# Mixture-of-experts steps of a decoder layer: two half blocks side by side on TensorE, results in rows of their own, the down bias inside the step

## The chip, the cores and the metric

The kernel runs on one core of a Trainium2 chip. The metric is the device time of one execution in microseconds; the timed runs are given by their median. The profile is of one execution that the hardware profiler recorded. Its span runs from the first to the last instruction, and the execution's own time is a little longer than the span.

## The reference

One decoder layer on 8 sequences of 112 tokens (896 tokens, width 512), all in fp32: causal self-attention with 16 heads of 128, a linear cross-attention over 375 context rows, and a mixture of 8 experts with the 2 best taken for each token. Each part is followed by a layer norm over the sum with its input. What the change touches is the last part:

```python
logits = h @ router_weight.T + router_bias
top_vals, top_idx = jax.lax.top_k(logits, TOP_K)          # TOP_K = 2, E = 8
top_w = jax.nn.softmax(top_vals, axis=-1)
scores = jnp.zeros_like(logits).at[jnp.arange(T)[:, None], top_idx].set(top_w)
gate_up = jnp.einsum('th,ehj->etj', h, gate_up_proj) + gate_up_proj_bias[:, None, :]
gate = jnp.minimum(gate_up[..., ::2], LIMIT)
up = jnp.clip(gate_up[..., 1::2], -LIMIT, LIMIT)
act = (up + 1.0) * gate * jax.nn.sigmoid(gate * ALPHA)
expert_out = jnp.einsum('eti,eih->eth', act, down_proj) + down_proj_bias[:, None, :]
out = jnp.einsum('te,eth->th', scores, expert_out)
...
x = _layernorm(x + out, axis=-1)
```

The inputs are drawn from a fixed seed, so the number of tokens that each expert gets is fixed as well.

## The kernel before

The 896 tokens are 7 tiles of 128 rows. Attention runs first (to about 530 us of the span). Then cross-attention is woven together with routing: for a batch b the cross-attention is finished, and `close(t)` (L956) projects a tile of tokens (xops), normalizes it (LN, with a square root on ACT) and routes it. `route` (L503) transposes the tile (x2T), forms the logits (lps), takes the best two on DVE, counts with a triangular matrix (cps) at which row of the expert's region each token goes, and scatters the token twice into `store`, a DRAM array with 896 rows for each expert. A row of `store` (516 words) holds the 512 values, the first expert's number (XF), the score difference (XD), the second score (XS) and the token's number (XK).

`keep_scores` (L576) builds for each tile the sum of the token and the score-weighted down bias: a transpose by matmul (sTps), a matmul with the biases (dbps), a DVE add (sum), and a store into the DRAM array `total`.

`list_blocks` (L610) works out on DVE, with some 18 to 22 small operations, which blocks of 128 rows of `store` the next steps take, and from which expert. It runs three times: after 5 tiles for 3 steps, after 6 tiles for 2 steps, and after all for 16 steps (`LISTS`, 21 steps in all). `es` is the expert, `eb` the same in integers with the block's number and, for late steps, whether the expert differs from the step four before.

An expert step s takes one block of 128 rows. Its parts, in the order of the final loop (L1209):
- `project(s, 0)`: 4 matmuls of 128x512 with the gate weights, called gups(s,0) below; DVE adds the bias (gu), takes the minimum, ACT does the sigmoid (sg).
- the transposes of step s-1's activation (aT, copied out by ACT) and of step s+1's block (bT, copied by ACT), with `start(s+1)`, a few small DVE operations.
- `project(s, 1)`: the same with the up weights, gups(s,1); three more DVE operations finish the activation g(s).
- `down(s-1)`: 4 matmuls with the down weights (yps), ACT copies the result to y, and POOL scatters y into `total` with an accumulating DMA.

There are four weight sets ("lanes", `NQ`) of three slabs of 1 MB (gate, up, down). Step s uses lane s % 4; `fetch_weights(s+3)` on SP's queue follows `down(s-1)` and is skipped where the expert hasn't changed (from step 9 on). `fetch_tokens(s+3)` on POOL's queue loads the block xblk, right after `start(s+1)`.

The order on PE, DVE, ACT and SP is the one in which the program is written (`manual_schedule`); each engine takes its instructions in that order. `tick()` advances the generators `close` and `keep_scores` by one piece, which weaves their pieces between the steps.

The tail: after step 15's result is scattered, SP loads `total` back in 7 tiles (xn), `close_tiles` normalizes them on DVE and ACT and writes them out. Tokens of the last five steps (`LATE`) are gathered from `total`, completed with y (`close_steps`), normalized and scattered into the output; `find_again` (L1180) finds on PE and DVE which tokens appear in two late steps, so that only the last one is written. The last step's result is completed in PSUM with a matmul over step 19's y (`finish`).

Of the kernel before, what the change touches and what calls it, by code (L numbers as in the profile page):

```python
# [19 lines left out]
P = 128  # L20
# [13 lines left out]
NQ = 4  # L34


LISTS = ((5, 3), (6, 2), (NT, 16))
STEPS = 21
LATE = 5
LN_EPS = 1e-5  # L40
# [5 lines left out]
def decoder_layer(ctx: ExitStack, tc: tile.TileContext, t_in: dict, out: bass.AP):  # L46
# [41 lines left out]
    def counting(name: str, shape, pattern):  # L88
# [27 lines left out]
    place = [  # L116
        counting(f"place{n}", [P, n, E], [[1, n], [0, E]]) for _, n in LISTS[:-1]
    ]
    late = LISTS[-1][1]
    place.append(  # L120
        counting(
            "place_late",
            [P, late // NQ, NQ, E],
            [[1, late // NQ], [late // NQ, NQ], [0, E]],
        ).rearrange("p i q e -> p (i q) e")
    )
# [12 lines left out]
    total = dram.tile([T + P, D], F32, name="total")  # L139
# [5 lines left out]
        base=T,  # L145
        channel_multiplier=1,
        allow_small_or_imprecise_dtypes=True,
    )

# [14 lines left out]
    def clear(n: int):  # L164
# [6 lines left out]
        else:  # L171
            nc.sync.dma_start(out=store[E * T :, :], in_=blank)
            nc.sync.dma_start(out=total[T:, :], in_=blank[:, :D])
# [325 lines left out]
    db = const.tile([E, D], F32, name="db")  # L499
    nc.scalar.dma_start(out=db, in_=t_in["db"])  # L500
    rows = const.tile([P, NT, 2], I32, name="rows")

    def route(t: int):  # L503
# [70 lines left out]
        return first, both  # L574

    def keep_scores(t: int, first, both):  # L576

        sco = small.tile([P, E], F32, tag="sco", name=f"sco_{t}")
        yield
        nc.vector.tensor_scalar_mul(sco, both, xe[:, t, XS : XS + 1])  # L580
        nc.vector.scalar_tensor_tensor(
            sco, first, xe[:, t, XD : XD + 1], sco, ALU.mult, ALU.add
        )
        yield
        yield
        yield
        sps = bank(f"sTps_{t}", "aux")
        nc.tensor.matmul(sps[:E, :P], sco, ident, start=True, stop=True)
        sT = small.tile([E, P], F32, tag="sT", name=f"sT_{t}", bufs=2)
        nc.scalar.copy(sT, sps[:E, :P])  # L590
        yield
        yield
        dps = bank(f"dbps_{t}", "aux")
        nc.tensor.matmul(dps, sT, db, start=True, stop=True)
        first_sum = side.tile([P, D], F32, tag="sum", name=f"sum_{t}")
        nc.vector.tensor_add(first_sum, xn[:, t, :], dps)
        yield
        yield
        put = nc.sync.dma_start(out=total[t * P : (t + 1) * P, :], in_=first_sum)
        if t == NT - 1:  # L600
            tc.declare_no_dep(put.ins, group="early", reason="tokens of other tiles")
# [83 lines left out]
    with tc.tile_pool(name="cross", bufs=2) as cr:  # L685
# [211 lines left out]
        def fetch_weights(s: int):  # L897
            for fetched in fetch_in_parts(s):
                pass
# [416 lines left out]
```

## Time and profile before

| what | us |
|---|---|
| median of 3 runs (988.66 to 990.53) | 990.17 |
| the profiled execution's own time | 985.63 |
| its span | 984.0 |
| first expert matmul starts | 721.59 |
| step 18 of 21 starts (third from the end) | 932.6 |
| last matmul of step 20's up projection ends | 962.9 |
| last normalized rows ready on DVE | 976.7 |

How to read it: the profile's parts are counted from the span's start. "Busy" of PE counts overlapping matmuls once. A group line gives engine, operation, output and inputs by the program's names, then the count, the busy time and the mean duration. A matmul in fp32 appears as two records. A line of the timeline gives start, length, engine, line, operation and how many records were merged into it.

The DMA queues in brief: q1 is SP's (98.28 MB), q0 is POOL's (15.75 MB). In the 40 slices of the page the DMA engines are near full from about 713 to 812 us.

### The profile page before, as it was taken

The page shows a single profiled execution, that of the slowest core. Times are in us where ns is not written, and L with a number is a line of the kernel's source. Part 1 is how long each engine was busy: PE and PEld are TensorE (multiplying, and loading weights), DVE is VectorE, ACT ScalarE, POOL GpSimd, SP SyncE. Part 2 cuts the span into 40 slices and gives each one's busy share as a digit, 9 for nine tenths or more (in the row PEclk, how much of TensorE's full clock was granted, in tenths as well). Part 3 has the DMA queues.
Part 4 walks back from the last instruction along what each step waited for, and adds up shares of the span by engine and source line. Part 5 has one row for each costly group of instructions (what it writes and reads, how often), then busy time and mean ns, then how long its engine had stood idle before and what let it go on. Part 6 is the DMA issues. An engine that isn't in the chain of part 4 may idle for free.

```text
span 984.0 us, 10556 instructions
## 1 busy us (share of the span) xinstructions
PE 949.3 (96%) x3847; PEld 490.5 (50%) x3847; DVE 461.0 (47%) x1020; ACT 244.7 (25%) x430; POOL 185.2 (19%) x235
## 2 busy tenths in 40 slices
PE   7998999999999999999999999999889999999994
PEld 3455644466445654654555454445444444444442
DVE  1356511145213551556421757667785433333484
ACT  1132311033102321332222233333223211211132
POOL 3133300031101322211002212221111212111132
PEclk9999999999999999999999999999999999999998
DMA  8991004102011001030100111120599997692432
GB/s 337 363 343 44 1 1 171 43 5 82 0 43 43 1 1 43 30 119 0 32 1 1 32 54 43 53 65 33 193 376 335 340 393 200 218 330 43 97 88 81
DMA packets 33845, 115.08 MB, mean 117 GB/s; under 512 B 3846, under 2 KB 8006, under 8 KB 26241
## 3 DMA queue, kind: packets, MB, share of 16 engines
q1 hardware_dynamic: 26784, 98.28, 27.2%
q0 software_dynamic: 6336, 15.75, 6.5%
q8 instruction: 31, 0.51, 0.2%
q10 hardware_dynamic: 672, 0.36, 0.1%
q14 instruction: 22, 0.17, 0.1%
HBM read 115.83 MB, written 29.01 MB: 147 GB/s over the span
## 4 chain that ended last, share of the span: by engine, by line
PE 84%; DVE 9%; issue 3%; ACT 2%; POOL 1%; DMA 1%; POOLq 0%; DVEq 0%; SPq 0%; ACTq 0%
PE gups L1061 14%; PE ops L237 10%; PE yps L1087 7%; PE vps L327 6%; PE zps L435 3%; PE xqps L877 2%; PE xgps L877 2%; PE sps L387 2%; DVE z L850 2%; PE xops L237 1%; PE pps L427 1%; PE aT_ps L982 1%; PE bT_ps L982 1%; DVE p L412 1%; PE sumps L812 1%
## 5 line engine op out<-in xcount | busy, mean ns | idle before, releaser
L1061 PE MATMUL gups<-slab,bT 128*128 128x512 f32 x336 | 153.2, 599 | 2.5 <-ACT bT L986 2.5
L1061 PEld LDWEIGHTS gups<-slab,bT 128*128 128x128 f32 x336 | 62.6, 192 | 73.0 <-issue 69.4
L237 PE MATMUL ops<-slab,zT 128*128 128x512 f32 x224 | 97.9, 593 | 0.0
L1069 DVE TENSOR_TENSOR gu<-gups,biases 128x512 f32<-128x512 f32 x42 | 29.0, 691 | 116.6 <-PE gups L1061 116.4
L1087 PE MATMUL yps<-slab,aT 128*128 128x512 f32 x168 | 76.0, 595 | 2.3 <-ACT aT L986 2.3
L237 PEld LDWEIGHTS ops<-slab,zT 128*128 128x128 f32 x224 | 42.1, 190 | 50.2 <-issue 49.5
L275 POOL TENSOR_TENSOR ws<-slab 128x256 f32<-128x256 f32 x16 | 11.8, 738 | 281.7 <-PE qk_5c L291 83.0
L327 PE MATMUL vps<-slab,x0T 128*112 128x512 f32 x128 | 58.7, 613 | 1.0 <-DVE x0T L187 0.8
L1101 POOL DMA_INDIRECT total<-y,nums x19 | 30.7, 1618 | 135.0 <-ACT y L1098 61.1
L1087 PEld LDWEIGHTS yps<-slab,aT 128*128 128x128 f32 x168 | 31.3, 190 | 40.5 <-issue 37.1
L244 DVE TENSOR_TENSOR xn<-xn,ops 128x512 f32<-128x512 f32 x28 | 19.2, 685 | 55.4 <-PE ops L237 55.4
L435 PEld LDWEIGHTS zps<-pT,v 112*128 112x128 f32 x256 | 33.5, 192 | 12.3 <-issue 11.1
L442 DVE COPY zT<-zps 128x448 f32<-128x448 f32 x32 | 20.0, 624 | 39.8 <-PE zps L435 39.8
L327 PEld LDWEIGHTS vps<-slab,x0T 128*112 128x112 f32 x128 | 22.9, 184 | 31.4 <-issue 29.7
L411 DVE TENSOR_REDUCE nm<-p 112x4 f32<-112x448 f32 x32 | 19.7, 616 | 30.8 <-POOL p L401 30.8
L1098 ACT COPY y<-yps 128x512 f32<-128x512 f32 x20 | 11.7, 584 | 87.8 <-issue 79.8
L435 PE MATMUL zps<-pT,v 112*128 112x112 f32 x256 | 33.4, 273 | 0.0
L1073 ACT ACTIVATE sg<-gu 128x512 f32<-128x512 f32 x21 | 13.2, 630 | 70.6 <-DVE gu L1071 53.0
L237 PE MATMUL xops<-slab,gate 128*128 128x512 f32 x56 | 25.8, 603 | 4.1 <-DVE gate L852 3.4
L395 ACT ACTIVATE p<-sps 112x448 f32<-112x448 f32 x32 | 17.4, 544 | 45.6 <-PE sps L387 45.6
L565 POOL DMA_INDIRECT store<-xn,rows x14 | 14.0, 1000 | 75.7 <-DVE count L627 48.2
L387 PE MATMUL sps<-k,q 128*112 128x112 f32 x256 | 28.0, 262 | 0.0
(799 smaller groups left out, 1616.5 us busy)
## 6 DMA issues: line engine op xcount, KB each, us to landing
slab<-in_wg_dram SPq DMA_DIRECT2D x21, 1024.0 KB
slab<-in_wu_dram SPq DMA_DIRECT2D x21, 1024.0 KB
slab<-in_wd_dram SPq DMA_DIRECT2D x21, 1024.0 KB
store<-slab SPq DMA_DIRECT2D x8, 1806.0 KB
biases<-gubs SPq DMA_DIRECT2D x21, 512.0 KB
cT<-in_ctxT_dram SPq DMA_DIRECT2D x8, 750.0 KB
xblk<-store POOLq DMA_DIRECT2D x21, 258.0 KB, 7.7
slab<-in_wq_dram SPq DMA_DIRECT2D x4, 1024.0 KB
```

The source lines that it names most:

```text
L237: nc.tensor.matmul(ps, aT[:, c, t * P : (t + 1) * P], w[:, c, :], start=(c == 0), stop=(c == C - 1),)
L327: nc.tensor.matmul(ps[:S, :], xT[:, c, b * S : (b + 1) * S], w[:, c, :], start=(c == 0), stop=(c == C - 1),)
L387: nc.tensor.matmul(ps[:S, i * S : (i + 1) * S], qk["q"][:, rows], qk["k"][:, rows], start=True, stop=True,)
L411: nc.vector.tensor_reduce(nm, p, AX.X, ALU.max, negate=True)
L435: nc.tensor.matmul(zps[:, i * S : (i + 1) * S], v[:, half * 4 + i, hl * DH : (hl + 1) * DH], pT[:, i * S : (i + 1) * S], start=True, stop= ...
L442: nc.vector.tensor_copy(zT[:, hl, half * HALF : (half + 1) * HALF], zps[:, :HALF])
L850: nc.vector.reciprocal(zf, zf)
L877: nc.tensor.matmul(ps[:, :HALF], w[:, c, g * P : (g + 1) * P], xT[:, c, cols], start=(c == 0), stop=(c == C - 1),)
L1061: nc.tensor.matmul(ps, st["bT"][:, c, :], st["w"][k][:, c, :], start=(c == 0), stop=(c == C - 1),)
L1069: nc.vector.tensor_add(a, ps, st["bias"][:, k * I : (k + 1) * I])
L1087: nc.tensor.matmul(ps, st["aT"][:, c, :], st["wd"][:, c, :], start=(c == 0), stop=(c == C - 1 and s < STEPS - 1),)
L1101: put = nc.gpsimd.indirect_dma_start(out=total, out_offset=bass.IndirectOffsetOnAxis(ap=st["num"], axis=0), in_=y, in_offset=None, compute ...
```

## The change

The steps become 18: 5 early ones with whole blocks (as before), 8 paired steps, and 5 late ones with whole blocks. A paired step takes two half blocks of 64 rows, possibly of two experts: half 0 in rows 0 to 63, half 1 in rows 64 to 127, with two lanes of weights, (1,2) or (3,0) in turn. Each matmul of 128 stationary columns becomes two of 64, one for each half, that write the lower and the upper half of the PSUM bank's rows. `list_blocks` now runs four times: the first two as before, then twice in a row after the last tile, for the five late whole blocks and for the paired halves (whole blocks are those that are more than half full; the rest are counted in halves).

`keep_scores` and `total` go. In their place the DRAM array `parts` has two rows for each token, one for each of its experts, plus 128 for padding; each step writes its result by a plain scatter into a row of its own (num = token + 896 x "is first expert"), and the token itself is added where it is the first expert. The down bias of the step's experts is loaded (`fetch_down_bias`) and enters y on DVE: y = bias x score + PSUM, then y = token x first + y (`add_token`); the copy on ACT goes. All of `parts` is cleared in attention (15 blocks of 256 KB instead of one). At the end SP loads 14 tiles (xn and `seconds`) after step 12, and `close_tiles` adds the two. Late steps gather the other expert's row.

Loads follow lanes: `fetch_inner(s)` loads gate and up weights and the biases for step s, `fetch_down(s)` the down weights; below inner(s) and down(s). `fetch_next(s, ...)` loads what the lanes of step s need next. `fetch_tokens(s+3)` moves behind `down(s-1)`, with two loads of 64 rows in a paired step. In step 0, `close` of the last tile moves from behind the second projection to behind the first.

The diff, cut to its core:

```diff
-LISTS = ((5, 3), (6, 2), (NT, 16))
-STEPS = 21
+LISTS = ((5, slice(0, 3)), (6, slice(3, 5)), (NT, slice(13, 18)), (NT, slice(5, 13)))
+EARLY, PAIRED, STEPS = 5, 13, 18
 LATE = 5
+LANES = [(s % NQ,) for s in range(EARLY)]
+LANES += [((1, 2), (3, 0))[s % 2] for s in range(PAIRED - EARLY)]
+LANES += [(1,), (2,), (3,), (0,), (1,)]
...
-    total = dram.tile([T + P, D], F32, name="total")
+    parts = dram.tile([2 * T + P, D], F32, name="parts")
...
-            nc.sync.dma_start(out=total[T:, :], in_=blank[:, :D])
+            nc.sync.dma_start(
+                out=parts.rearrange("(n p) d -> p n d", p=P),
+                in_=blank[:, :D].unsqueeze(1).broadcast_to([P, 2 * NT + 1, D]),
+            )
...
-    def keep_scores(t: int, first, both):
...
+        def fetch_down_bias(s: int):
+            downs[s] = side.tile([P, D], F32, tag="down_bias", name=f"down_bias_{s}", bufs=2)
+            for i, (e, _) in experts_of.pop(s).items():
+                on, _ = part_of(s, i)
+                nc.sync.dma_start(
+                    out=downs[s][on],
+                    in_=t_in["db"][bass.ds(e, 1), :].broadcast_to([on.stop - on.start, D]),
+                )
...
             elif t == NT - 1:
                 list_blocks(2)
-            later.append(keep_scores(t, *first_both))
+                list_blocks(3)
...
             for c in range(C):
-                nc.tensor.matmul(
-                    ps,
-                    st["bT"][:, c, :],
-                    st["w"][k][:, c, :],
-                    start=(c == 0),
-                    stop=(c == C - 1),
-                )
+                for rows_, q in parts_of(s):
+                    nc.tensor.matmul(
+                        ps[rows_],
+                        st["bT"][:, c, rows_],
+                        slab[3 * q + k][:, c, :],
+                        start=(c == 0),
+                        stop=(c == C - 1),
+                    )
...
-            nc.scalar.copy(y, ps)
+            nc.vector.scalar_tensor_tensor(
+                y, downs.pop(s), st["score"], ps, ALU.mult, ALU.add
+            )
+            add_token(y, st)
             st["y"] = y
             if s < STEPS - 2:
-                put = nc.gpsimd.indirect_dma_start(
-                    out=total,
+                nc.gpsimd.indirect_dma_start(
+                    out=parts,
                     out_offset=bass.IndirectOffsetOnAxis(ap=st["num"], axis=0),
                     in_=y,
                     in_offset=None,
-                    compute_op=ALU.add,
-                )
+                )
             if s == STEPS - LATE - 1:
                 for t in range(NT):
-                    nc.sync.dma_start(
-                        out=xn[:, t, :], in_=total[t * P : (t + 1) * P, :]
-                    )
+                    for k, to in ((1, xn), (0, seconds)):
+                        nc.sync.dma_start(
+                            out=to[:, t, :],
+                            in_=parts[k * T + t * P : k * T + (t + 1) * P, :],
+                        )
...
             for t in range(NT):
+                nc.vector.tensor_add(xn[:, t, :], xn[:, t, :], seconds[:, t, :])
                 closing_stats(t, xn[:, t, :])
...
             if st:
                 project(s, st, 0)
+                if s == 0:
+                    settle(0)
+                    chains.append(close(NT - 1))
                 tick()
+            if s - 2 >= STEPS - LATE:
+                before_last = steps[s - 2]
+                nc.vector.tensor_add(before_last["sum"], before_last["sum"], before_last["y"])
...
-                if s >= 1 and s + 3 < STEPS:
-                    ahead_x.append(fetch_tokens(s + 3))
             if st:
                 project(s, st, 1)
-                if s == 0:
-                    settle(0)
-                    chains.append(close(NT - 1))
                 tick()
                 if s == 0:
-                    next(third)
-                    ahead_w.append(fetch_weights(3))
+                    fetch_down(2)
+                    fetch_inner(3)
+                    fetch_down(3)
+
+                if s not in (1, PAIRED):
+                    fetch_next(s, fetch_inner)
+                if s == 2:
+                    fetch_next(1, fetch_inner)
...
             if before_:
                 down(s - 1, before_)
                 tick()
-                if s - 1 + NQ < STEPS:
-                    ahead_w.append(fetch_weights(s - 1 + NQ))
+                if s == PAIRED:
+                    fetch_next(s, fetch_inner)
+                fetch_next(s - 1, fetch_down)
+                if s + 1 < STEPS:
+                    fetch_down_bias(s + 1)
+                if s + 3 < STEPS:
+                    ahead_x.append(fetch_tokens(s + 3))
```

## The prediction

> **What bounds the kernel now.** I read the page's totals first, then TensorE's order of time (the timeline of PE) around the expert steps, then the busy time by stretch, then the orders of ACT and DVE where a wait shows.
>
> ```profile
> span 984.0 us, 10556 instructions
> PE 949.3 (96%) x3847; PEld 490.5 (50%) x3847; DVE 461.0 (47%) x1020; ACT 244.7 (25%) x430; POOL 185.2 (19%) x235
> ...
> DMA packets 33845, 115.08 MB, mean 117 GB/s; under 512 B 3846, under 2 KB 8006, under 8 KB 26241
> ...
> PE 84%; DVE 9%; issue 3%; ACT 2%; POOL 1%; DMA 1%; POOLq 0%; DVEq 0%; SPq 0%; ACTq 0%
> ```
>
> TensorE is busy 96% of the span and carries 84% of the chain that ended last. So PE work that goes is time that goes, unless another engine is late in its place. One expert step, and the one place where column strips are used already:
>
> ```profile
> 716.25 1.03 PE L812 MATMUL sumps<-values,kf 125*32 125x33 f32 x96
> ...
> 758.18 1.12 PE L594 MATMUL dbps<-db,sT 8*128 8x512 f32 x2
> 759.23 3.70 PE L1087 MATMUL yps<-slab,aT 128*128 128x512 f32 x8
> 762.77 3.60 PE L1061 MATMUL gups<-slab,bT 128*128 128x512 f32 x8
> 766.20 0.60 PE L982 MATMUL aT_ps<-ident,gu 128*128 128x128 f32 x4
> 766.64 0.60 PE L982 MATMUL bT_ps<-ident,xblk 128*128 128x128 f32 x4
> 767.08 3.60 PE L1061 MATMUL gups<-slab,bT 128*128 128x512 f32 x8
> 770.51 3.60 PE L1087 MATMUL yps<-slab,aT 128*128 128x512 f32 x8
> ```
>
> By the starts a step is 3.43 + 0.44 + 0.44 + 3.43 + 3.43 = 11.18 us with no gap. A matmul is two records; 512 columns are (3.60 - 0.59) / 7 = 430 ns each. The sumps matmuls write four 32-row strips with 33 columns each: in a row these would be 430 x 33 / 512 = 27.7 ns apart, but they start (1.03 - 0.20) / 95 = 8.7 ns apart. Four strips thus ran 3.2 at a time, in fp32, each with its own moving data.
>
> ```profile
> 745.00:757.00 12.00, 12.00 (x47) 6.48 (x46) 5.55 (x21) 3.46 (x7) 1.66 (x1) 1.00 1.02 402
> 876.00:921.00 45.00, 45.00 (x132) 21.85 (x131) 16.83 (x44) 8.70 (x16) 8.07 (x7) 1.00 0.36 88
> 944.00:956.00 12.00, 12.00 (x37) 5.97 (x36) 10.55 (x28) 7.03 (x11) 3.56 (x3) 1.00 0.37 88
> 956.00:984.00 28.00, 15.43 (x42) 6.66 (x40) 14.64 (x34) 5.75 (x10) 8.77 (x8) 0.89 0.31 93
> ```
>
> The columns are PE, PEld, DVE, ACT, POOL busy, clock, DMA share, GB/s. The steps are PE-bound throughout; DMA is saturated at 402 GB/s early and idle late; DVE is nearly full (10.55 of 12) just before the end.
>
> **What the skill says.** TensorEngine Tiling (Key Properties): tiles work in parallel, and a change of tiling mode drains TensorE. The sumps line agrees on the first; its neighbours start without a visible gap, so the drain is under 0.1 us here. TensorE: Matmul & The Clock Gate (Part 3): three column tiles at N=512 gave 2.38x, matmuls are strict FIFO. If FIFO holds, a pair's low record waits for its own half and one slot of 0.43 us is lost per run. DMA: Bandwidth & Descriptors (Rules for kernel authors): two transfers to partition halves serialize, so halving xblk and the biases saves nothing; no run here shows it.
>
> **The change, part by part.** All in the profiled execution's time (span 984.0, run 985.63); the runs' median 990.17 is 4.5 us above it, and I carry the difference over.
>
> (a) Before the first expert matmul (721.6). keep_scores goes: per tile one sTps (0.31 us on PE) and one dbps (1.05), and a DVE sum (0.68). Up to 691 PE is full (157.5 of 161 us) and three tiles' worth goes: 3 x 1.36 = 4.1. Between 691 and 721.6 the chain runs through DVE as well: one sum 0.7, one dbps 1.05, one sTps partly 0.2. First gups at 715.6: -6.0. The larger clear of parts (15 blocks of 256 KB, in attention) lies under a DMA share near 0.1: nothing; if a weight load waited, some 10 us of queue, with two heads (16 heads take 530 us) before the next load.
>
> (b) Steps 0 and 1. Here the last tile's close moves ahead of the second gups, and list_blocks runs twice in a row.
>
> ```profile
> 755.48 1.28 ACT L558 ACT_TABLE_LOAD   x1
> 756.77 0.20 ACT L558 ACTIVATE ex<-d 128x1 f32<-128x1 f32 x1
> 756.88 0.57 ACT L986 COPY aT<-aT_ps 128x512 f32<-128x512 f32 x1
> ...
> 754.65 0.16 DVE L543 TENSOR_TENSOR at<-cps,upto 128x8 f32<-128x8 f32 x1
> ...
> 757.66 0.16 DVE L627 TENSOR_TENSOR count<-upto 128x8 f32<-128x8 f32 x1
> ...
> 761.15 0.15 DVE L995 CAST nums<-xblk 128x1 int32<-128x1 f32 x1
> ```
>
> Routing takes 757.66 - 754.65 = 3.0 us of DVE; the list 3.5 us for 18 operations, 0.194 each. Walk of the new order: gups(0,0) 715.6; xops waits for gate (724.2 - 5.0 = 719.2), then bT(1) and gups(0,1) end at 726.6. DVE finishes list_blocks(1) at 724.9, then gu(0), adds xops and normalizes: with two ACT table loads of 1.28 in between, xn is ready at 730.4. PE waits 3.8 (before: 2.55 at this place). x2T, gups(1,0), lps, aT, bT, gups(1,1) end at 739.5 = c. Now in DVE's queue stand gu(1) 2.8, routing 3.0, 45 list operations 8.7, y(0) 1.45, and only then gu(2,0) 1.1: c + 17.0. ACT's sg(2) (table 1.28 + 0.63) waits for that, and aT(1) (0.57) stands behind sg(2): c + 19.5. PE's own work (cps, yps(0), gups(2,0), aT, bT, gups(2,1)) lasts until c + 11.4. So yps(1) waits 8.1 us and starts at 759.0, against 759.23 before. The 6 us of (a) are given back. Bounds on this wait: 5 to 10.
>
> (c) From yps(1) to the third step from the end. Before: 759.2 to 932.6. After: yps(1) 3.43, then 12 steps x 11.18 = 134.2, keys 0.2. The three steps less are 33.5 us. Terms not in the trace:
> - Column halves: 8 paired steps with 12 pairs each. From below: fully side by side, 0. From above: one after the other, 8 x 12 x 0.86 = 82. By the sumps line each strip's matmul cost about 5.5 ns over its stream, 1% at 512 columns. I take one lost FIFO slot a step: 8 x 0.43 = 3.4.
> - Tokens: fetch_tokens(s+3) now stands behind y(s-1) and its scatter on POOL, 11 us later than before. y +1.7, scatter issue +1.2, first half's fetch +1.2, second +1: issued by +5. The view of the tile xblk, from issue to landing:
>
> ```profile
> DMA to landing us min/median/max: 2.9/7.7/12.1
> ```
>
> bT(s+3) is due at 11.18 + 3.9 = +15.1, so the median has 2 us to spare and the worst is 2 us late. Between 0 and 10 us in all; I take 1.5 us.
> - Weights: the seeded inputs route 260, 280, 188, 216, 264, 172, 200, 212 rows to the experts. Before: 13 experts are loaded (9 unconditional, 4 on change; the page's 7,604 packets of 8 KB and over agree, 384 an expert plus 20 earlier slabs). After, by the lists: 5 + 9 + 5 = 19, of 3.15 MB. Seven come within steps 5 to 8, whose slabs come free one step ahead. At 345 GB/s left for this queue, wu and wd of steps 7 and 8 land about when they are due: 0 to 7 us, I take 2.
> - Two new DVE operations a step (bias and token into y, 0.73 each) replace ACT's copy (0.58): DVE goes to some 6.3 of 11.2 us, hidden. The plain scatter instead of an accumulating one costs POOL no more than its 1.6 us.
> Third step from the end: 759.0 + 3.4 + 134.2 + 0.2 + 3.4 + 1.5 + 2 = 903.7.
>
> (d) The tail. Before: 932.6 to 984.0 = 51.4. After, DVE gets seven xn + seconds adds (0.69 each), two operations for each y and sum + y at once. In steps 15 and 16 its queue sums to 17.5 and 13.8 us against 22.4 of PE. Further, SP's 14 xn and seconds loads wait for step 12's scatter, take 3.67 MB / 300 GB/s = 12 us (290 GB/s in the stretch 929 to 935, where seven such loads run before), and behind them stand inner(17), down(15), down(16) and then the down bias of step 14: it lands 22 us into step 15, where y(14) wants it at 16.5. DVE stands 5.6 us, and behind it gu(16,0), sg, aT(15). Adding DVE's queue from there: g(16) at 35, sg(17) at 43.7, yps(16) 44.3 to 47.7, last scale at 57.3, against 44.1 before: 64.6 to the end. Bounds: 56 (bias in time, DVE covered) to 70.
>
> **Sum.** 903.7 + 64.6 = 968.3, 15.7 less than 984.0. On the median: 990.17 - 15.7 = 974.5 us.
>
> **Rivals.**
> 1. As summed: 974.5, own range 964 to 986. Chance 0.69.
> 2. Slower: the halves do not overlap for 512 columns. Place: gups and yps of the eight paired steps. Price: up to 82 - 3.4 = 79 us, 1053; decided once a pair costs over (15.7 + 3.4) / 82 = 23% more than one full matmul. For: no 64-column half is in the trace, and 33-column strips are short. Against: 3.2 streams at once were sustained there. Chance 0.12, spread between 990 and 1053.
> 3. Transfers bind in the paired steps: tokens 1 us late in each (8) and weights 4 more: 986. For: DMA share 1.02 at 402 GB/s early, 6 experts more. Against: the load is light in steps 9 to 12. Chance 0.11.
> 4. The tail's queue is absorbed (14 loads early, bias in time): 8 to 11 us better, 964. Against: DVE's sum alone fills two steps. Chance 0.08.
>
> **Numbers.** What can be told from no change is 0.2%, 2 us. Faster: 0.69 x 0.98 + 0.11 x 0.6 + 0.08 = 0.82, taken at 0.80; same 0.04; slower 0.16 (rival 2 and the end of 3). The range 961 to 997 leaves out most of rival 2 and a little below.
>
> **What would show it.** Right: gups of a paired step with 16 records in about 3.5 to 3.9 us; 18 steps; no dbps; a PE wait of some 8 us for ACT aT L1022 before the second yps; DVE over 0.9 busy in the last 45 us and PE waiting there on aT. Wrong: 16 records in 6.9 us; PE waits on xblk or slab in steps 5 to 9 above 10 us together; or a tail no longer than before.

## The result, and the profile after

The changed kernel is slower: 995.71 us median against 989.06 for the kernel before, ratio 1.0072 with a 95% interval of 1.0054 to 1.009. Forecast were 974.5 us and "faster". The profiled execution (993.77 us) has a span of 992.2 us (before 984.0, summed in the prediction 968.3). Cut into four stretches, the span shows where the forecast and the chip part. Steps begin with their first gups; step 3 is the fourth of the 18.

| stretch (us) | before | predicted | after | after less predicted |
|---|---|---|---|---|
| start to first gups | 721.6 | 715.6 | 720.9 | +5.3 |
| first gups to start of step 3 | 41.2 | 46.8 | 47.1 | +0.3 |
| step 3 to third step from the end | 169.8 (15 steps) | 141.3 (12 steps) | 155.1 | +13.8 |
| from there to the end | 51.4 | 64.6 | 69.2 | +4.6 |

The page after, in the same lines as were read before:

```profile
span 992.2 us, 10895 instructions
PE 925.1 (93%) x3915; PEld 468.3 (47%) x3915; DVE 481.1 (48%) x1053; ACT 226.9 (23%) x394; POOL 173.8 (18%) x239
...
DMA packets 39653, 142.35 MB, mean 143 GB/s; under 512 B 4438, under 2 KB 8598, under 8 KB 29744
...
PE 61%; DVE 13%; issue 12%; DMA 9%; ACT 2%; POOL 1%; POOLq 0%; SPq 0%; DVEq 0%; ACTq 0%
```

TensorE lost 24.2 us of work (949.3 to 925.1), but the span grew by 8.2: TensorE's share of the chain that ended last fell from 84% to 61%, and DMA's rose from 1% to 9%. The bytes grew by 27.3 MB. Packets of 8 KB and over are 39,653 - 29,744 = 9,909, which is 2,305 more than before: six experts at 384 packets each are 2,304, as the lists said (19 loads against 13).

TensorE's order of time after (start, length, group, and in brackets the idle time before it with what ended it):

```profile
720.85 6.17 PE L1120 MATMUL gups<-slab,bT 128*128 128x512 f32 x8
...
761.99 6.09 PE L1147 MATMUL yps<-slab,aT 128*128 128x512 f32 x8 [5.95 <-ACT aT L1022]
...
815.77 3.65 PE L1120 MATMUL gups<-slab,bT 128*64 128x512 f32 x14 [1.04 <-DMA slab<-in_wg_dram]
...
822.85 3.65 PE L1120 MATMUL gups<-slab,bT 128*64 128x512 f32 x14 [1.41 <-DMA slab<-in_wu_dram]
829.40 3.97 PE L1147 MATMUL yps<-slab,aT 128*64 128x512 f32 x16 [2.90 <-ACT aT L1022]
...
846.37 6.08 PE L1147 MATMUL yps<-slab,aT 128*64 128x512 f32 x13 [3.75 <-DMA slab<-in_wd_dram]
...
864.19 3.60 PE L1120 MATMUL gups<-slab,bT 128*64 128x512 f32 x16
867.72 0.65 PE L1018 MATMUL aT_ps<-ident,gu 128*128 128x128 f32 x4
868.21 0.60 PE L1018 MATMUL bT_ps<-ident,xblk 128*128 128x128 f32 x4
868.74 3.65 PE L1120 MATMUL gups<-slab,bT 128*64 128x512 f32 x16
872.23 3.60 PE L1147 MATMUL yps<-slab,aT 128*64 128x512 f32 x16
875.66 3.60 PE L1120 MATMUL gups<-slab,bT 128*64 128x512 f32 x16
...
956.21 0.77 PE L1249 MATMUL keys<-sums,allones 128*128 128x128 f32 x2 [13.89 <-DVE closing L217]
956.77 5.90 PE L1147 MATMUL yps<-slab,aT 128*128 128x512 f32 x8
```

Three things are to be seen. First, the lines from 864.19 to 875.66 are one undisturbed paired step: 11.47 us, and 16 records of 64 columns take 3.60 to 3.65 us, what 8 records of 128 took before. The halves run side by side; a paired step costs 0.29 us more than a whole one (11.18). Second, the waits: 5.95 us before the second yps (forecast 8.1), then steps 7 and 8, from 813.71 to 851.55, which take 19.8 and 18.1 us, since TensorE waits there for gate, up and down weights and for aT, and 13.9 us in step 16. Third, groups of eight matmuls that take 6.1 instead of 3.6 us: TensorE at about half its clock, mostly after such a wait. The mean clock granted is 0.58 while gups(0,0) runs (from 720.85), 0.59 for yps(1), 0.50 for the thirteen records from 846.37 and 0.60 for the yps from 956.77.

The stretches (PE, PEld, DVE, ACT, POOL busy, clock, DMA share, GB/s), first after, where 820 to 880 stands once whole and once in its two halves, then before:

```profile
760.00:820.00 60.00, 56.97 (x198) 23.65 (x199) 25.97 (x54) 8.78 (x16) 10.66 (x16) 0.94 1.02 346
820.00:880.00 60.00, 51.81 (x228) 18.79 (x226) 22.71 (x49) 6.37 (x12) 7.85 (x11) 0.94 0.90 280
820.00:850.00 30.00, 21.81 (x89) 7.89 (x88) 9.43 (x22) 3.18 (x6) 2.10 (x3) 0.92 1.02 312
850.00:880.00 30.00, 30.00 (x143) 10.90 (x140) 13.28 (x27) 3.18 (x6) 5.75 (x8) 0.96 0.79 247
880.00:935.00 55.00, 54.17 (x203) 23.44 (x202) 32.01 (x83) 7.96 (x15) 7.05 (x9) 1.00 1.00 385
```

```profile
820.00:880.00 60.00, 60.00 (x173) 28.92 (x172) 20.07 (x51) 11.46 (x21) 12.43 (x11) 1.00 0.75 245
880.00:935.00 55.00, 55.00 (x161) 26.81 (x160) 21.88 (x58) 10.87 (x20) 8.06 (x7) 1.00 0.36 80
```

The DMA engines, slack from 880 on before, are full after (share 0.99 to 1.03) from 760 to 850, in which steps 7 and 8 wait, and again from 880 to 940; from 850 to 880 the share is 0.79. In the tail DVE's own order shows the late bias:

```profile
939.33 0.16 DVE L1259 TENSOR_TENSOR again<-again,twice 128x3 f32<-128x3 f32 x1
946.60 0.75 DVE L1158 SCALAR_TENSOR_TENSOR y<-down_bias,score,yps 128x512 f32<-128x512 f32 x1 [7.11 <-DMA down_bias<-in_db_dram]
```

### The profile page after: what moved, and what is told of

Its sections match the earlier page's. It is cut to its first block, busy times and chain, and to the rows that moved or that the text cites. A ratio compares the mean times of both kernels' runs of the same rounds, so it can differ in the third digit from the quotient of the medians.

```text
span 992.2 us, 10895 instructions
## 1 busy us (share of the span) xinstructions
PE 925.1 (93%) x3915; PEld 468.3 (47%) x3915; DVE 481.1 (48%) x1053; ACT 226.9 (23%) x394; POOL 173.8 (18%) x239
## 2 busy tenths in 40 slices
DMA packets 39653, 142.35 MB, mean 143 GB/s; under 512 B 4438, under 2 KB 8598, under 8 KB 29744
## 4 chain that ended last, share of the span: by engine, by line
PE 61%; DVE 13%; issue 12%; DMA 9%; ACT 2%; POOL 1%; POOLq 0%; SPq 0%; DVEq 0%; ACTq 0%
PE ops L254 10%; PE vps L344 6%; DMA parts<-y,nums 5%; PE zps L452 3%; PE xqps L888 2%; PE xgps L888 2%; DVE z L861 2%; PE sps L404 2%; PE xops L254 1%; DMA down_bias<-in_db_dram 1%; PE pps L444 1%; DVE p L429 1%; PE sumps L823 1%; DVE kf L783 1%; PE kvps_0a L769 1%
## 5 line engine op out<-in xcount | busy, mean ns | idle before, releaser
L1120 PE MATMUL gups<-slab,bT 128*64 128x512 f32 (+1 forms) x416 | 136.2, 603 | 2.6 <-DMA slab<-in_wu_dram 1.4
L1147 PE MATMUL yps<-slab,aT 128*64 128x512 f32 (+1 forms) x208 | 74.4, 650 | 14.5 <-ACT aT L1022 9.9
L1120 PEld LDWEIGHTS gups<-slab,bT 128*64 128x64 f32 (+1 forms) x416 | 48.7, 160 | 73.2 <-issue 68.8
L1128 DVE TENSOR_TENSOR gu<-gups,biases 128x512 f32<-128x512 f32 x36 | 24.8, 689 | 73.6 <-PE gups L1120 56.6
L1147 PEld LDWEIGHTS yps<-slab,aT 128*64 128x64 f32 (+1 forms) x208 | 27.1, 173 | 55.9 <-issue 38.5
L1164 POOL DMA_INDIRECT parts<-y,nums x16 | 16.5, 1033 | 158.8 <-DVE y L1185 144.2
L1158 DVE SCALAR_TENSOR_TENSOR y<-down_bias,score,yps 128x512 f32<-128x512 f32 x17 | 12.7, 747 | 32.6 <-PE yps L1147 24.6
L412 ACT ACTIVATE p<-sps 112x448 f32<-112x448 f32 x32 | 17.4, 544 | 45.6 <-PE sps L404 45.6
```

The costliest lines, as they stand in the source:

```text
L1120: nc.tensor.matmul(ps[rows_], st["bT"][:, c, rows_], slab[3 * q + k][:, c, :], start=(c == 0), stop=(c == C - 1),)
L1128: nc.vector.tensor_add(a, ps, st["bias"][:, k * I : (k + 1) * I])
L1147: nc.tensor.matmul(ps[rows_], st["aT"][:, c, rows_], slab[3 * q + 2][:, c, :], start=(c == 0), stop=(c == C - 1 and s < STEPS - 1),)
```

## The experiments

All medians, with the ratio to the kernel before run on the same chip. m1, m2, a1 and t3 leave out work that the result needs; they only price it.

| run | us | ratio, 95% interval |
|---|---|---|
| m1_no_weights_7_8 | 979.26 | 0.9916, 0.9884 to 0.9947 |
| m2_no_biases_7_8 | 988.33 | 0.9995, 0.9976 to 1.0015 |
| b1_bias_before_up | 999.48 | 1.0112, 1.0076 to 1.0148 |
| m3_reversed | 980.92 | 0.9898, 0.9859 to 0.9937 |
| t1_bias_before_sums | 995.26 | 1.0071, 1.0046 to 1.0096 |
| t2_bias_sums_weights | 992.15 | 1.0011, 0.9987 to 1.0035 |
| s1_lists_apart | 994.16 | 1.0057, 1.0034 to 1.008 |
| a1_no_keep_scores | 980.91 | 0.9921, 0.9892 to 0.995 |
| c1_three_orders | 978.91 | 0.9894, 0.9851 to 0.9937 |
| c2_adds_on_pool | 977.0 | 0.9875, 0.9835 to 0.9915 |
| d1_filled_waits | 981.17 | 0.9908, 0.9871 to 0.9944 |
| e1_orders_pool_filled | 987.27 | 0.9998, 0.9978 to 1.0019 |
| f1_sums_later | 977.92 | 0.9879, 0.9857 to 0.9902 |
| t3_no_second_adds | 978.46 | 0.9889, 0.9868 to 0.9911 |
| g1_short_fillers | 972.62 | 0.9837, 0.9816 to 0.9859 |

### The loads of steps 7 and 8

Weights left out (m1, in `fetch_inner` and in `fetch_down`):

```diff
                     e, cond = chosen[i]
+                    if s in (7, 8):
+                        continue
```

> The changed kernel without the loads of gate, up and down weights for steps 7 and 8 (three experts by the lists, 9.4 MB); the biases are still loaded, and steps 7 and 8 compute with the weights left in their slabs. Theory A (the bytes of the weights bind the first paired steps): steps 7 and 8 fall from 19.8 and 18.1 to 11.5 to 12.5 us each, DVE's waits on the biases go as well, and the time falls by 13 to 16 us to about 981. Rival E (the paired steps wait for something else, the biases or the tokens): steps 7 and 8 stay above 15 us. The gap between step 16 and 17 stays at 28 us in any case.

Measured: 11.47 and 11.48 us for the two steps, together 14.9 less; the time is 16.5 below the changed kernel's. In the stretch view of this run:

```profile
760.00:820.00 60.00, 57.55 (x206) 24.17 (x208) 27.98 (x63) 10.16 (x18) 11.12 (x17) 0.94 0.95 317
820.00:880.00 60.00, 60.00 (x296) 21.96 (x294) 28.14 (x63) 8.62 (x17) 9.43 (x13) 1.00 0.70 246
```

From 820 to 880 TensorE is busy throughout, the DMA share 0.70 instead of 0.90. Without these 9.4 MB nothing stops steps 7 and 8. The waits for the biases went with them, so m1 alone does not divide the 14.9 us between weights and biases.

Biases left out (m2, the same two lines in the loop over the biases), and biases issued earlier (b1):

```diff
+            load(0, "wg")
+            if not EARLY <= s < PAIRED:
+                load(1, "wu")
             for i in parts_:
...
+            if EARLY <= s < PAIRED:
+                load(1, "wu")
```

> The changed kernel without the loads of the gate and up biases for steps 7 and 8 (at most four times 256 KB); the weights are loaded as before, and the two steps add the biases left in their rows. Theory A (the weights' bytes bind; the biases are late because they stand behind them): the waits of 2.9 and 3.75 us for ACT's aT go, but TensorE then waits on the slabs instead; steps 7 and 8 together fall from 37.9 us by 0 to 4 us. Rival E (the place of the biases behind the weights is what costs): steps 7 and 8 fall by 7 to 10 us together, since the two aT waits and one yps at half clock go.

> The changed kernel (lanes in their first order) with the gate and up biases of the paired steps issued between the gate and the up weights instead of behind both; nothing is left out. Theory E (the place of the biases behind the weights costs: without them steps 7 and 8 fell by 8.4 us): the two aT waits (2.9 and 3.75 us) and the yps at half clock go, steps 7 and 8 together fall from 37.8 to 30 to 33 us, the time by 4 to 8 us. Theory A alone (only bytes count, and what goes at the biases comes back at the up weights): 36 us or more, and the time stays within 2 us of the changed kernel's.

Without the biases the two steps fell by 8.4 us to 29.4, as theory E had it; with the biases ahead of the up weights they still took 36.3. The wait of 2.9 us for aT was gone, but TensorE now waited 2.9 us for gate, 1.5 for up and 2.5 for down weights (1.0, 1.4 and 3.8 in the changed kernel: the 3.75 us that both expectations give to aT were a wait for down weights, by the line at 846.37). The time did not fall (999.48; its interval overlaps with the changed kernel's). So giving the biases this earlier place gains nothing: what goes at the biases comes back at the weights. Left out in m2 were 142.35 - 141.56 = 0.79 MB, 2 to 3 us at the 280 to 346 GB/s of that stretch; the rest of the 8.4 would be the steps behind a late bias (DVE, ACT, aT) and one yps at half clock, which is argued and not shown. Whether loads into 64 of the 128 rows are slower for their size was not measured.

The lanes' halves in reverse order (m3), which changes no result, only when which expert is due:

```diff
-            pattern=[[1, (PAIRED - EARLY) // 2], [PAIRED - EARLY, 2], [0, E]],
-            base=half * (PAIRED - EARLY) // 2,
+            pattern=[[-1, (PAIRED - EARLY) // 2], [PAIRED - EARLY, 2], [0, E]],
+            base=(half + 1) * (PAIRED - EARLY) // 2 - 1,
```

> The changed kernel with each lane's four half blocks taken in the reverse order. The halves and the results are the same; by the lists three experts fewer are loaded for steps 7 and 8 (one instead of three for step 7 and none, since a lane now starts with the expert it has most halves of), three instead of one for steps 11 and 12, and none for step 13: 18 experts instead of 19. Theory A (bytes due in steps 7 and 8 bind): these two steps fall from 37.8 us to 23 to 25, and what was gained is kept, since the loads of steps 11 and 12 come when the queue is light: 980 us (977 to 984). Rival F (the queue is short of bytes over the whole stretch from step 5 to step 16, so that a wait only moves): steps 7 and 8 fall as much, but waits on slabs of 8 us or more appear in steps 11 to 16 and the time stays at 988 or more.

Measured: steps 7 and 8 take 11.47 us each, no step from 7 to 15 takes more than 11.74, and the stretch from step 3 to step 15 is 138.0 us (155.1 in the changed kernel, 141.3 forecast). The time falls by 14.8 us. Two things changed at once, the spread of the loads (three experts were due in two steps) and their number (one less, 139.20 MB); no run parts them.

This profile had luck as well. Its first gups came only at 728.6, behind groups at half clock (below), and step 3 at 775.6, 7.7 us later than in the changed kernel, so that the loads had more time. In the seven other runs with the reversed halves (all of which change other orders too) step 3 starts between 761.0 and 768.8, waits for weights stand again, above all at the end of step 6 (2.2 us or more) and in steps 11 to 13, and the stretch to step 15 lasts 144.4 to 150.6 us. That is still less than the 153.6 to 157.1 us of the five programs with all loads and the first order. So theory A holds for steps 7 and 8; F as it was put falls (no such waits in m3, and 981 instead of 988 us), but transfers still hold these steps once they come earlier.

### The tail

The 14 sums' loads behind bias and weights (t1), or the bias first, then sums, then weights (t2):

```diff
                 if s == STEPS - LATE:
+                    fetch_down_bias(s + 1)
+                    load_sums()
+                    fetch_next(s, fetch_inner)
                 fetch_next(s - 1, fetch_down)
```

> The changed kernel with the 14 loads of xn and seconds issued on SP after the down bias of step 14 instead of before the weights of steps 15 to 17. Theory A (the late bias makes the tail long): DVE's wait of 7.1 us at y(14) goes, TensorE's wait of 13.9 us before the keys matmul shrinks to 5 us or less and the yps after it runs at 3.6 instead of 5.9 us; the tail from step 15's start (69.2 us) becomes 57 to 61, the time 8 to 12 us less than the changed kernel's (995.7 to about 986). Rival B (DVE's own work in the tail binds, the bias only sits in front of it): DVE is busy over 0.95 in steps 15 and 16 and the tail stays at 66 us or more. Rival C (xn and seconds are now late instead): a wait of 5 us or more on xn or seconds appears at the sums' adds on DVE and the tail gains less than 4 us.

> The changed kernel with the down bias of step 14 issued on SP ahead of the 14 loads of xn and seconds, which stay ahead of the weights of steps 15 to 17. Theory A (in the tail the bias's place costs, and the earlier variant failed since it put 5 MB of weights ahead of the sums): no wait of DVE on down_bias and none over 1 us on seconds; y(14) starts at once, the wait of 13.9 us before the keys matmul falls to 5 to 8, because DVE's own queue between gu(15,1) and the closing roots still lasts that long; the tail falls from 69.2 to 60 to 63 us and the time by 5 to 9 us. Rival B (DVE's own queue is all that counts): the tail stays at 67 or more though the bias's wait is gone.

In t1 DVE's wait only changed its name, rival C:

```profile
938.29 0.69 DVE L1215 TENSOR_TENSOR xn<-xn,seconds 128x512 f32<-128x512 f32 x1 [7.74 <-DMA seconds<-parts]
```

The weights now ahead of the sums are bytes too, and the tail stayed at 70.2 us. In t2 neither is late, and TensorE's wait halves:

```profile
956.19 0.76 PE L1249 MATMUL keys<-sums,allones 128*128 128x128 f32 x2 [6.77 <-DVE closing L217]
```

The tail is 61.4 us (from 69.2), in the forecast span of 60 to 63, but the median fell by only 3.6 us (forecast 5 to 9). Step 14 took 17.4 us in this execution and 12.6 in the changed kernel's profile: yps(13) waited 4.0 us for its down weights and then took 5.4 instead of 3.6. The same wait stood in s1, m2 and b1 (3.5 to 4.1; 1.6 in t1); so the changed kernel's one profile, with 0.8, was lucky there. The line in t2, then in the changed kernel:

```profile
924.91 5.37 PE L1155 MATMUL yps<-slab,aT 128*128 128x512 f32 x8 [4.00 <-DMA slab<-in_wd_dram]
```

```profile
919.51 3.67 PE L1147 MATMUL yps<-slab,aT 128*128 128x512 f32 x8 [0.83 <-DMA slab<-in_wd_dram]
```

The long step 14 also flatters t2's tail, since bias and sums had nearly 5 us more to land before step 15: in c1 (below), with the same order of loads and a step 14 of 11.5 us, DVE waits 3.5 us for the bias again and the tail is 66.3 us. Counted from the start of step 14, t2 needs 78.8 us to the end, the changed kernel 81.8, and s1, m2 and b1, which also had the long step 14, 83.7 to 84.4. So the bias's place is worth some 3 to 6 us, not the 7.8 that the tails alone suggest.

Three runs on top of c1 (below) ask what fills the remaining wait. The add of the gathered sum moved back (f1), the seven adds left out as well (t3), or put on POOL (c2):

```diff
-            if s - 2 >= STEPS - LATE:
-                before_last = steps[s - 2]
-                nc.vector.tensor_add(before_last["sum"], before_last["sum"], before_last["y"])
...
                 project(s, st, 1)
+                if s - 2 >= STEPS - LATE:
+                    add_last(s)
```

> The kernel with the three orders changed, and the add of the gathered sum and y behind the gated activation of the same step instead of before it; all adds on DVE. If the gather counts, DVE's wait of 3.5 us no longer stands before the activation of step 16: the gap from step 16 to step 17 falls from 25.1 to about 21.5 us and the time from 978.9 to about 975. If DVE's queue alone counts, the gap stays above 24 us.

> The kernel beside it with the seven adds xn + seconds left out (the second expert's part of the tokens is missing in the output; the loads stay). If DVE's queue is the path, seven times 0.7 = 4.9 us go from the wait before the keys matmul and from the gap from step 16 to step 17 (to about 16.5 us), and the time falls by 4 to 5 us against the kernel beside it. If the queue has slack, under 2 us.

> The kernel with the three orders changed, and in the tail the seven adds xn + seconds on POOL instead of DVE, and the adds of sum and y behind the gated activation instead of before it. Theory A (from step 15 on the path is DVE's queue: seven adds of 0.69, and the wait of 3.5 us for a gather, stand before the activation of step 16): the wait of 11.7 us before the keys matmul falls to 2 to 5 us, the gap from step 16 to step 17 from 25.1 to 15 to 18 us, the time from 978.9 to 969 to 973. Rival H (POOL's adds, at about 1.46 us each by the 0.73 us that 256 columns take there, hold up the scatters and gathers on POOL, so that the end waits for them): the time stays at 977 or more, with waits of DVE on sums or xn.

f1: the gap from step 16 to 17 fell from 25.1 to 21.7 us as expected; the time moved by 1 us, within the intervals, where 4 were expected. t3: the gap is 19.0 instead of the 16.5 expected, and the time does not fall (978.46 against f1's 977.92), so by the fork that was set DVE's queue has slack. DVE waits elsewhere in t3:

```profile
940.87 0.69 DVE L1286 TENSOR_TENSOR sums<-sums,y 128x512 f32<-128x512 f32 x1 [4.43 <-DMA sums<-parts,others]
...
959.62 0.75 DVE L1335 SCALAR_TENSOR_TENSOR sums<-down_bias,score,sums 128x512 f32<-128x512 f32 x1 [3.73 <-DMA sums<-parts,others]
```

and POOL's order in t3 shows what for:

```profile
926.49 1.00 POOL L1174 DMA_INDIRECT parts<-y,nums  x1 [8.66 <-DMA slab<-in_wg_dram]
934.43 1.00 POOL L1193 DMA_INDIRECT sums<-parts,others  x1 [6.95 <-DMA parts<-y,nums]
941.61 0.98 POOL L1174 DMA_INDIRECT parts<-y,nums  x1 [6.18 <-DMA sums<-parts,others]
```

Scatter and gather follow each other through `parts`: POOL waits 6.95 us from this scatter to the gather and 6.18 from there to the next scatter (2.88 and 2.02 for the two gathers after that), and the scatter of 926.49 itself starts late. A reading that fits is that DVE's queue and this chain are about equally long, so that taking 4.9 us from one gains nothing; no run shortened the chain.

c2 put the adds on POOL, and the wait moved to step 15 (20.7 us to step 16). DVE's order in c2, then POOL's:

```profile
923.26 0.14 DVE L1032 COPY keys<-xblk 128x1 f32<-128x1 f32 x1
923.32 5.20 DVE L1034 TENSOR_TENSOR is_first<-xblk,es 128x1 f32<-128x1 f32 x1
928.56 0.22 DVE L1038 SCALAR_TENSOR_TENSOR score<-xblk,is_first 128x1 f32<-128x1 f32 x1
```

```profile
923.57 4.93 POOL L1353 TENSOR_TENSOR xn<-xn,seconds 128x512 f32<-128x512 f32 x4
```

An operation on one column, 0.15 us elsewhere, took 5.20 us while POOL ran four adds (and 5.21 beside the same four adds in e1). The Trainium skill states the cause (SBUF — State Buffer, Who interferes with whom): a DVE instruction with two SBUF inputs contends with a GpSimd instruction that reads SBUF; this one has two, xblk and es, and the trace agrees in that it stands until the four adds are over. Neither A nor H had that; with 977.0 us, 11.6 us from step 16 to 17 and no wait of DVE on sums above 1.6 us, c2 does not decide between them.

### The start

The second list behind gu(2,0) (s1: two `yield` lines between `list_blocks(2)` and `list_blocks(3)`):

> The changed kernel with the second of the two lists after the last tile (20 operations on DVE, about 4 us) behind gu(2,0) instead of before y(0). Theory A (DVE's order holds yps(1)): TensorE's wait of 5.95 us for ACT's aT before yps(1) falls below 2.5 us, yps(1) no longer takes 6.09 us but 3.6 to 4, and step 3 starts 5 to 7 us sooner after the first gups (47.1 to about 41). If that gain stays to the end, the time is 990. Rival D (transfers bind steps 5 to 8, so that what is gained before is waited away there): step 3 starts sooner, but the waits of steps 7 and 8 grow by the same 5 to 6 us and the end moves by less than 2 us.

The wait before the second yps fell to 2.5 us, but a wait of 3.3 us for tile 6's transposes and a half-clock gups took most of that back: 45.6 us to step 3 (47.1). The median fell by 1.6. Step 3 began 1.6 us sooner and step 15 no sooner (at 923.4 against 923.0), the outcome of rival D, but not in its place: steps 7 and 8 took 34.4 us (37.8), step 13 began 4.4 us sooner, and the long wait for step 13's down weights, which the changed kernel's profile happened to lack, took that back.

keep_scores' arithmetic out of the kernel before (a1):

```diff
-        sps = bank(f"sTps_{t}", "aux")
-        nc.tensor.matmul(sps[:E, :P], sco, ident, start=True, stop=True)
...
-        nc.vector.tensor_add(first_sum, xn[:, t, :], dps)
+        first_sum = xn[:, t, :]
```

> The kernel before without the arithmetic of keep_scores: the sums with the down bias are left out (the two matmuls, the copy on ACT, three operations on DVE for each tile); the plain token rows are stored into total at the same place. As the prediction had it, the first gups comes 5 to 6 us sooner (721.6 to 716) and the time falls by 7 to 8 us. Rival G (TensorE waits for DVE and ACT in that stretch, so that its shorter list only makes it wait): the first gups moves by less than 2 us, the time by less than 4 us.

The time fell by 9.4 us against 990.3 beside it, so the part is worth at least what step (a) and the later dbps were put at. But its first gups starts at 720.83, only 0.8 sooner. TensorE came to the last two waits earlier and waited longer there (3.2 for gate, before 2.9; 2.5 for the transposes, before 2.2), and lps to gups ran at half clock behind them. By step 3 4.4 us are gained, at the end of the span 6.2.

Three orders at once (c1 = m3, t2 and s1), then with fillers (d1, and e1 = c2's edits and d1's), then f1 with shorter fillers (g1):

```diff
+    def warm(ps, n: int):
+        for _ in range(n):
+            nc.tensor.matmul(ps[:, :P], ident, ident, start=True, stop=True)
...
+            if tag == "xops" and t == NT - 2:
+                warm(ps, 10)
```

> The changed kernel with three changes of order at once: the lanes' half blocks reversed, the down bias of step 14 ahead of the sums, and the second list behind gu(2,0). Theory A: the three places are independent, so the gains add: 15 + 7 + 3 to 5 us, some 970 us (966 to 976), below the kernel before. Rival F (one shortage of transfer that waits move around in): the gains do not add, 980 or more.

> The kernel with the three orders changed, and with matmuls that nobody reads (128x128 by the unit matrix) in TensorE's waits: 24 before the projection of tile 5, 16 before the transposes of tiles 5 and 6, 16 before the second yps, 48 before the last keys. Theory K (after idle gaps TensorE runs at half its clock for about 5 us, and this is why the first gups came anywhere from 719.0 to 728.6 in runs of the same program): the first gups comes at 717 to 720, no group of eight matmuls takes 5 us or more between 700 and 770 us or after the last keys, and the time falls by 2 to 5 us against 978.9. Rival L (the half clock comes from elsewhere, load or temperature, whatever the gaps): groups at half clock remain as before, the time stays within 1.5 us.

> All of the two kernels beside it: three orders, adds on POOL, filled waits. If theories A and K hold and are independent, 966 to 970 us; if only one of them holds, 970 to 976.

> The kernel with the sums later, and shorter fillers in TensorE's waits of the start: 10, 8 and 12 matmuls of 128x128 before tile 5's projection and before the two tiles' transposes, 8 before the second yps (0.23 us each in the run before); none in the tail. Theory K (half clock after gaps): the first gups comes at 717 to 719.5, step 3 starts at 761 to 764, no group of eight matmuls takes 5 us or more in the start. Whether it shows at the end depends on the loads for steps 7 and 8: if they bind (theory F), the waits there grow by what was gained and the time stays within 1.5 us of the kernel with the sums later; if not, it falls by 2 to 4 us.

c1's gains do not add up: 978.9 lies between the 966 to 976 of theory A and the 980 of rival F. It has waits of 1.75 us for down and 2.3 for gate weights again, and 3.5 each for the down bias and a gather. Step 3 starts 9.5 us sooner than in m3's profile, step 15 only 3.0.

The twelve programs that are alike up to the first gups started it anywhere from 719.0 to 728.6 us. TensorE's order in the worst, m3:

```profile
710.63 6.56 PE L254 MATMUL xops<-slab,gate 128*128 128x512 f32 x8 [3.21 <-DVE gate L863]
...
728.61 6.12 PE L1120 MATMUL gups<-slab,bT 128*128 128x512 f32 x8
```

in c1, where the same wait costs nothing and a shorter one does:

```profile
707.61 3.67 PE L254 MATMUL xops<-slab,gate 128*128 128x512 f32 x8 [3.21 <-DVE gate L863]
...
760.96 5.37 PE L1157 MATMUL yps<-slab,aT 128*128 128x512 f32 x8 [2.49 <-ACT aT L1024]
```

and in g1, where matmuls that nobody reads stand in the wait:

```profile
703.66 2.40 PE L251 MATMUL xops<-ident 128*128 128x128 f32 x20
706.94 3.70 PE L260 MATMUL xops<-slab,gate 128*128 128x512 f32 x8 [0.88 <-DVE gate L871]
...
718.28 3.68 PE L1130 MATMUL gups<-slab,bT 128*128 128x512 f32 x8
...
757.43 3.70 PE L1167 MATMUL yps<-slab,aT 128*128 128x512 f32 x8 [0.71 <-ACT aT L1032]
```

With fillers no group of eight in the start takes over 3.7 us, in g1 as in d1 and e1, while each of the twelve programs has one of 5.8 us or more there: theory K. In g1 step 3 starts at 761.0 (f1: 762.5, the changed kernel: 767.9), and the time is 5.3 us below f1's (the two intervals overlap by 0.0002). The fillers' own part in this is smaller than 5.3 as far as the two profiles show: 1.5 us are gained by step 3, and 5.7 between step 3 and step 15, where f1 waits more for tokens, weights and aT, in steps 4, 8, 11 and 12 above all; why g1 does not is not shown. From the start of step 6 to that of step 7, where both wait for gate weights, it is 16.4 us, in f1 16.3.

The Trainium skill describes a mechanism (TensorE: Matmul & The Clock Gate, Part 1): the clock drops to half after an idle window of about 3.4 us, and the windows run free of the program. The traces agree with the second half: the same wait of 3.2 us for the gate costs the next group nothing in seven of the twelve programs, c1 among them, and 1.7 to 2.9 us in the five others (2.9 in m3). With the first they agree only in part, since waits shorter than that window are followed by half clock too: 2.49 us before the second yps in s1, c1, c2 and t3 (5.4 us for the yps), though not in f1 (3.70). In d1 the fillers were too many (5.52 us in a wait of 3.2; first gups at 722.4), and nothing was won; in e1, the worst miss of these runs (987.27 where 966 to 970 were expected), 48 fillers before the last keys took 10.9 us where the wait had become shorter, and DVE waited 6.2 us for keys: 22.1 us from step 16 to step 17, against 11.6 in c2.

g1 is faster than both kernels: 0.9837 of the kernel before.

## Why the prediction was wrong

The sign was wrong, and the size by 21 us. Taking its steps in order:

- **(a) before the first gups, -6.0.** Failed: -0.7 in the profile. The term "three tiles' worth, 4.1" did not come through: TensorE's work from 530 to 680 fell by 2.8 us, but at 676 it was only 1.3 us ahead, and it had waited 3.9 us for DVE before its xops (1.1 before). "Up to 691 PE is full" left these waits out. At full clock (c1) the first gups comes at 719.0, -2.6; the other 1.9 in the profile are half clock, which the prediction did not have at all.
- **(b) steps 0 and 1.** Right as a sum (46.8 forecast, 47.1), by errors that cancel: the waits were shorter than forecast (5.95 instead of 8.1 before yps(1), 0.87 instead of 3.8 before x2T), and gups(0,0) and yps(1) lost 2.5 each at half clock. That is luck.
- **(c) the middle.** Here the forecast failed. Column halves, at 3.4 (0 to 82): 8 x 0.29 = 2.3, right. (The 5.5 ns per strip named beside it does not come out of the sumps line, where four strips take 4 x 8.7 - 27.7 = 7.1 ns over one stream; the sum does not use it.) Tokens, at 1.5: no wait on xblk, 0. Weights, at 2 (0 to 7): this is the step that failed. The two steps alone lost 14.9, which m1 shows; that is more than the whole excess of 13.8 in this stretch. The loads were counted rightly (six experts more, seven in steps 5 to 8), and 22 MB at the 345 GB/s that were assumed are 64 us, which is the whole stretch from 768 to 833. So "about when they are due" had no margin, and two things then broke it: with the engines full (share 1.02) all queues together moved 312 GB/s from 820 to 850, less than the 345 assumed for SP's alone, and an arrival that was late cost more than its lateness, by the chain bias, gu, sg, aT (2.9 us before yps(6)) and by half clock (2.4 at yps(7)). How the 14.9 us divide among these is not shown. With the loads spread the middle is 138.0 us in m3's late execution, and 144.4 to 150.6 in the other seven, against the 141.3 forecast.
- **(d) the tail.** Right in its mechanism: the down bias was forecast 22 us into step 15 and came at 23.6, y(14) wanted it at 16.5 and did at 16.5. The size was 4.6 short, of which 2.3 are yps(15) at half clock; within the bounds of 56 to 70. By t2 the bias's place is worth 3 to 6 us.

Of the rivals, the third (transfers bind in the paired steps, chance 0.11) was the one, with weights where it had put tokens, and 15 us where it had 6. The point it missed, as did the main line, is that waits have a price of their own: behind four of them stood groups at half clock, which lost some 12 us in all (2.3 at lps to cps, and 2.5, 2.5, 2.4, 2.3 at gups(0,0), yps(1), yps(7), yps(15)), part of it inside the stretches named above; the kernel before shows one, gups(1,0) at 5.40, worth 1.8.

What stays open: how much of m2's 8.4 us is bytes; how much of m3's gain is the spread and how much the expert less; which of DVE's queue and the chain through `parts` a better tail must shorten first; how much of g1's 5.3 us the fillers give; and why the down weights of step 13 were 0.8 us late in one execution and 4 in others.

## What to carry to other kernels

When a change trades TensorE work for transfers, sum the bytes due in each stretch against the rate that the trace shows there, not against the best one: a load that lands "about when due" is a stall, and the order of work that decides when a load is due is cheap to change (14.8 us here for two lines). Compare several executions before a stretch is called cured: a late start alone can hide a shortage of transfers, as in m3 and t2. Price a new TensorE wait of 2.5 us or more at the wait plus up to 2.9 us of half clock (1.6 to 2.4 after each wait of 5.9 us here, and after waits of 2.5 and 3.2 us in some executions only), and if it cannot be removed, try filling it with unread matmuls, fewer than the wait holds. A late operand on a queue in strict order is cured only if what is put behind it is not needed as soon.

## What the runs showed of the hardware

- Two fp32 matmuls of 64 columns on the two column halves, with 512 elements each and different weights and inputs, ran side by side: 16 records in 3.60 to 3.65 us, 8 of 128 columns in 3.60 (changed kernel).
- POOL's adds of 128x512 took 1.23 to 1.27 us each, and a DVE operation on one column with two inputs from SBUF stood for 5.20 us beside four of them (0.15 elsewhere; c2, and 5.21 in e1). Beside such adds in c2 two operations on a tensor and a column stood as well, 1.26 us (gu, 128x512) and 1.21 (sums, 128x128), against 0.43 and 0.28 in t3.
- TensorE's wait of 5.9 us before the second yps was followed by a group at half clock in all seven programs that had it (5.30 to 6.09 us for the yps instead of 3.70), the wait of 2.5 us in four of five, and the wait of 3.2 us for the gate in five of twelve.
- A filler of 128x128 by the unit matrix took 0.23 us in a row of its own where 10 to 48 stood together (2.40 for 10 in g1, 10.88 for 48 in e1), two records each; a transpose of the same size, one record, took 0.11 (groups of four started 0.44 apart).
